# When a transposed input is turned and fetched: the feed-forward steps of an attention kernel, one step earlier

## The chip, the cores and the metric

The kernel runs on one core of one Trainium2 chip. The metric is the device time of the whole program in microseconds. A core has five engines that this text names as the profile does: PE (the matrix engine; PEld is its weight loads), DVE (the vector engine), ACT (the scalar engine), POOL (the general engine) and SP, whose only work here is to issue transfers. Each engine works through its own list of instructions in order.

## What is computed

The input `x` has the shape (2, 256, 128, 128): batch, time, frequency band, channel, all in 32-bit floats. Three residual layers follow each other, each behind a layer norm over the channels:

```python
xt = _ln(x, ln_t_w, ln_t_b).transpose(0, 2, 1, 3)
x = x + _mha(xt, t_wi, t_bi, t_wo, t_bo, H_T, cm).transpose(0, 2, 1, 3)
xf = _ln(x, ln_f_w, ln_f_b)
x = x + _mha(xf, f_wi, f_bi, f_wo, f_bo, H_F, bm)
xn = _ln(x, ln_n_w, ln_n_b)
h = jax.nn.gelu(xn @ w1.T + b1, approximate=False)
x = x + (h @ w2.T + b2)
```

The first attention runs over the 256 times of each band (causal mask), the second over the 128 bands of each time (a band mask of 16), both with four heads of 32. The feed-forward layer has 512 hidden units.

## The kernel before, in words

A test on the weights at the start picks one of two paths, and for these inputs it is `BoundedPath` (from line 877 on). Its work is cut into 384 *groups* of 512 tokens, each a tile of 128 partitions by four blocks of 128 channels: 128 groups of kind `OverTime` first, which write their result to an intermediate `x1` in device memory, and then 16 *runs*. A run is eight groups of kind `OverBands` and then eight of kind `FeedForward` on the same tokens; the middle result stays on the chip in a tile named `x2`.

The method `run` (line 1000) is a software pipeline written out by hand. It loops over a step number `n`; in each step it calls pieces of work of groups ahead of `n` and behind it. For a feed-forward group `k` the pieces are these:

- `statistics` (mean and variance, DVE) in step k-5, `root` (the inverse deviation, POOL) in step k-4.
- `normalize` and `turn` (line 1049) in step k-2. `normalize` is four DVE instructions that write `xh`; `turn` (line 504) is one DVE instruction that transposes 32 by 32 blocks into `z`, and four transfers that store `z` into a small buffer in device memory, `turned`.
- `fetch` (line 1047) in step k-1: one transfer that reads `turned` back as `xnT`, the transposed, normalized input with the channels on the partitions.
- `first_half` in step k: hidden units 0 and 1 (`hp`, two matrix products on `xnT`); `second_half`, later in step k: hidden units 2 and 3. In the first feed-forward step of a run, which the code calls the *turn*, the second half follows the first at once.
- `weigh` in step k+1: the 16 products `zp` that add up the hidden units. `divide`, in the same step: one DVE addition `res<-zp,res`, and on every second group the store to `out`.

For an `OverBands` group `k` the same pieces stand in other steps: `normalize` and `turn` in step k-3 (line 1050), `fetch` in k-2 (line 1046), the products for queries, keys and values in k-1, the scores `sp` in step k, `rp` and `op` in k+1, `yp` in k+2. Below, *band step b* and *feed step f* are the steps with `n` at the b-th band group and the f-th feed-forward group of a run, both counted from 0; *feed group f* is named in the same way.

A group's tokens come in with `load`, called for group n+11 at the head of each step (line 1024). Four groups share one tile `x` of four blocks. The transfers of the tile are issued by its first two groups, two transfers each (lines 943 and 974).

Three things decide when a piece really runs:

- The instructions of PE, DVE, ACT and POOL are pinned to the order of the program (`InOrder`, line 862). So the step that a piece is called in fixes its neighbours on its engine.
- The transfers are not pinned. The framework's scheduler puts them in an order of its own into the one list that SP works through, and an SP instruction that must wait holds all those behind it.
- Tiles come from rings of buffers: three for `xnT`, two each for `xh` and `z`, three for `turned`, four for `x`, and eight banks for what PE writes, handed out in turn. A writer waits until the last reader of the buffer's previous tile has done.

Of the kernel before, what the change touches and what calls it, by code (L numbers as in the profile page):

```python
# [25 lines left out]
NT = 4  # L26
# [623 lines left out]
def rows_of(h):  # L650
    return slice(h * D, (h + 1) * D)
# [225 lines left out]
class BoundedPath:  # L877
# [53 lines left out]
    def groups(self, x, out):  # L931
        nc, k = self.nc, self.k
        B, T, FB, C = x.shape
        NC_T = T // P
        for b in range(B):
            for f0 in range(0, FB, GA):
                held = {}


                def load(g, f0=f0, b=b, held=held):  # L940
                    if g == 0:
                        self.quad(held, "x", 4)
                    for i in range(2 * g, min(2 * g + 2, NT)):
                        f = f0 + i // NC_T * NT
                        nc.sync.dma_start(held["x"][rows_of(i)], self.of_times(x[b], i, slice(f, f + NT)))

                def store(g, f0=f0, b=b, held=held):
                    for i in range(NT if g % 2 else 0):
                        f = f0 + i // NC_T * NT + g
                        nc.sync.dma_start(  # L950
                            self.of_times(k.x1[b], i, slice(f - 1, f + 1)), held["res"][rows_of(i), :, g - 1 : g + 1]
                        )

                def part(name, g, i=None, a=0, held=held):
                    if name == "res" and name not in held:
                        self.quad(held, "res", 2)
                    if i is not None:
                        return self.longer(held[name], i * NT + g, a)
                    return held[name][:, :, g]

                for g in range(NT):
                    yield OverTime(self, partial(part, "x", g), partial(part, "res", g), partial(load, g), partial(store, g))
        for b in range(B):
            for r0 in range(0, T, RUN):
                run = []
                for t0 in range(r0, r0 + RUN, GB):
                    held = {}


                    def load(g, t0=t0, b=b, held=held):  # L970
                        if g == 0:
                            self.quad(held, "x", 4)
                            self.quad(held, "x2", 2 * RUN // GB)
                        for i in range(2 * g, min(2 * g + 2, NT)):
                            nc.sync.dma_start(
                                held["x"][rows_of(i)].rearrange("q g t c -> q (g t) c"),
                                self.of_bands(k.x1[b], t0 + NT * i, NT),
                            )

                    def store(g, t0=t0, b=b, held=held):  # L980
                        for i in range(NT if g % 2 else 0):
                            nc.sync.dma_start(
                                self.of_bands(out[b], t0 + NT * i + g - 1, 2),
                                held["res"][rows_of(i), g - 1 : g + 1].rearrange("q g t c -> q (g t) c"),
                            )

                    def part(name, g, i=None, a=0, held=held):
                        if name == "res" and name not in held:
                            self.quad(held, "res", 2)
                        if i is not None:  # L990
                            return self.longer(held[name], g * NT + i, a)
                        return held[name][:, g]

                    run += [(g, part, load, store) for g in range(NT)]
                for g, part, load, _ in run:
                    yield OverBands(self, partial(part, "x", g), partial(part, "x2", g), partial(load, g))
                for g, part, _, store in run:
                    yield FeedForward(self, partial(part, "x2", g), partial(part, "res", g), None, partial(store, g))

    def run(self, x, out):  # L1000
        groups = list(self.groups(x, out))

        def do(n, *names):
            if 0 <= n < len(groups):
                for name in names:
                    getattr(groups[n], name)()
# [4 lines left out]
        def do_at(n, kind, *names):  # L1011
            if at(n, kind):
                do(n, *names)
# [1 line left out]
        A = RUN // NT  # L1015

        self.scalar.preload_act_table_set(EXP_SET)
        for n in range(-11, len(groups) + 2):
            feeds = [at(n - 2 + i, FeedForward) for i in range(5)]
            bands = [at(n - 2 + i, OverBands) for i in range(5)]  # L1020
            turn = feeds[2] and bands[1]
            old, new = (groups[i] if at(i, OverTime) else None for i in (n, n + 1))
            self.by_columns = at(n - 1, Attention)
            do(n + 11, "load")
            if bands[2] and feeds[1]:
                self.scalar.preload_act_table_set(EXP_SET)
            do_at(n + 4, FeedForward, "root")
            do(n, "first_half", "first_function", "first_mask")
            if old is not None or new is not None:
                time_scores(old, new)  # L1030
                b = self.banks
                Attention.place = dict(rp=b["b0"], op=b["b3"], yp=b["a1"], qp=b["a2"], kp=b["b1"], vp=b["b2"])
            else:
                Attention.place = {}
            if old is not None:
                old.second_weights(old.late)
            if new is not None:
                new.first_weights(new.early)
            if old is not None:
                old.second_weights(old.early)  # L1040
                old.mask_second()
                old.add(0)
            if turn:
                do(n, "second_half", "second_function")
            do_at(n + 3, OverTime, "fetch")
            do_at(n + 2, OverBands, "fetch")
            do_at(n + 1, FeedForward, "fetch")
            do_at(n + 5, OverTime, "statistics")
            do_at(n + 2, FeedForward, "normalize", "turn")
            do_at(n + 3, OverBands, "normalize", "turn")  # L1050
            do_at(n + 4, OverTime, "normalize", "turn")
            do_at(n + 5, FeedForward, "statistics")
            do(n - 1, "weigh")
            do(n - 1, "invert_exactly" if turn else "invert")
            if new is not None:
                new.first_weights(new.late)
                new.mask_first()
            if old is not None:
                old.add(1)
            if bands[2] or turn or old is not None:  # L1060
                do(n - 2, "output", "finish")
            do(n - 1, "divide")
            if not turn:
                do(n, "second_half", "second_function")
            if not bands[2]:
                do_at(n, FeedForward, "bias")
                do_at(n + A, OverBands, "bias")
                if at(n - 1, FeedForward) and at(n - 2, OverBands):
                    do_at(n + A - 1, OverBands, "statistics", "root")
                if not turn:  # L1070
                    do_at(n + A, OverBands, "statistics")
                    if not at(n, OverTime):
                        do_at(n + A, OverBands, "root")
            do_at(n + 2, OverTime, "queries_keys", "take_query", "take_key")
            do_at(n + 1, OverBands, "queries_keys", "take_query", "take_key")
            do_at(n + 5, OverTime, "root_by_scalar", "refine")
            if at(n - 1, OverTime):
                do_at(n + A - 1, OverBands, "root_by_scalar", "refine")
            do_at(n, OverTime, "bias")
            if not bands[2] and not turn and old is None:  # L1080
                do(n - 2, "output", "finish")
            do_at(n + 2, OverTime, "values", "take_values")
            do_at(n + 1, OverBands, "values", "take_values")
            if old is not None or new is not None:

                b = self.banks
                self.banks = dict(
                    a1=b["a1"], a2=b["a2"], b0=b["a0"], b3=b["a3"], a0=b["b0"], a3=b["b1"], b1=b["b3"], b2=b["b2"]
                )
# [69 lines left out]
```

## Time and profile before

The median of three runs is 2756.72 us (2755.34 to 2758.24). The profiled execution has a span of 2755.9 us.

| engine | busy us | share |
|---|---|---|
| PE | 2695.7 | 98% |
| DVE | 2288.9 | 83% |
| POOL | 1861.0 | 68% |
| ACT | 1843.3 | 67% |

| stretch | length us | PE busy | DVE busy |
|---|---|---|---|
| start, to 40 us | 40 | 10.18 | 20.94 |
| 40 to 880: over time | 840 | 835.99 | 807.64 |
| 880 to 2700: change of kind, and the runs | 1820 | 1801.75 | 1441.74 |
| end | 56 | 47.74 | 18.61 |

| transfer | count | KB each | median us to landing |
|---|---|---|---|
| turned<-z | 1536 | 64 | 2.0 |
| xnT<-turned | 384 | 256 | 2.8 |
| x<-in_x | 128 | 256 | 5.4 |
| x<-x (from `x1`) | 128 | 256 | 4.2 |
| out<-res | 256 | 128 | 2.4 |

The 128 groups over time take until about 980 us. The first feed-forward group of the first run starts at 1045.37 us, and from there on the runs follow each other at some 109 us each; the last one, with no bands of a further run in it, takes 56 us. Because the pieces are recorded by one helper, all of them carry line 872, and the rows of the profile are told apart by the names of their tiles. A matrix product of 32-bit floats is recorded twice, so the four products `hp` of a group are eight records.

### The profile page before, as it was taken

How to read it: one execution, taken by the hardware profiler on the slowest of the kernel's cores; microseconds unless marked ns; L12 is line 12 of the kernel's file. 1: busy time of each engine (PE TensorE's matmuls, PEld its weight loads, DVE VectorE, ACT ScalarE, POOL GpSimd, SP SyncE). 2: the span in 40 equal slices, each digit the busy share in tenths (PEclk: the TensorE clock that was granted, in tenths of full speed). 3: DMA queues.
4: the chain of work that ended last, by engine and by line, in shares of the span. 5: the costliest groups of instructions: out<-in, count | busy, mean ns of one | idle time of the engine just before them, and what ended most of it. 6: DMA issues, size and time to landing. Idle time of an engine off the chain costs nothing.

```text
span 2755.9 us, 105739 instructions
## 1 busy us (share of the span) xinstructions
PE 2695.7 (98%) x43522; PEld 1880.6 (68%) x43522; DVE 2288.9 (83%) x6727; ACT 1843.3 (67%) x3600; POOL 1861.0 (68%) x2169
## 2 busy tenths in 40 slices
PE   5999999999999999999999999999999999999998
PEld 3666766667666666676676766766766767667666
DVE  5999999999999987868778778687687796776874
ACT  3888888888888874655746646557456465465563
POOL 2878878788887876666657566666566665665762
PEclk9999999999999999999999999999999999999999
DMA  5565555555555564444443544544444445344333
GB/s 126 135 154 135 148 156 141 142 154 144 148 149 144 134 157 105 109 129 108 121 127 105 129 108 109 132 115 115 129 107 122 111 114 130 103 117 113 87 97 86
DMA packets 471310, 343.84 MB, mean 125 GB/s; under 512 B 43296, under 2 KB 405152, under 8 KB 470816
## 3 DMA queue, kind: packets, MB, share of 16 engines
q1 hardware_dynamic: 469568, 335.92, 47.3%
q8 instruction: 344, 5.64, 0.9%
q14 instruction: 150, 1.23, 0.2%
q10 hardware_dynamic: 1248, 1.05, 0.1%
HBM read 169.03 MB, written 167.77 MB: 122 GB/s over the span
## 4 chain that ended last, share of the span: by engine, by line
PE 82%; DVE 11%; DMA 4%; issue 1%; SPq 1%; POOL 1%; ACT 0%; DVEq 0%
PE zp L872 17%; PE hp L872 16%; PE sp L872 10%; PE op L872 7%; PE rp L872 7%; PE vp L872 7%; PE qp L872 6%; PE kp L872 6%; PE yp L872 6%; DVE xh L872 2%; DVE vy L872 2%; DMA xnT<-turned 2%; DVE u L872 1%; DVE stats L872 1%; DVE res L872 1%
## 5 line engine op out<-in xcount | busy, mean ns | idle before, releaser
L872 ACT ACTIVATE hT<-hp,b 128x512 f32<-128x512 f32 x512 | 350.2, 687 | 553.0 <-PE hp L872 542.1
L872 POOL TENSOR_SCALAR_AFFINE_SELECT pf<-pf 128x512 f32<-128x512 f32 x768 | 476.9, 635 | 274.8 <-ACT pf L872 248.6
L872 DVE TENSOR_SCALAR xh<-x,mv,rstd 128x160 f32<-128x160 f32 x1536 | 596.2, 430 | 14.1
L872 PEld LDWEIGHTS zp<-w2T_sb,hT 128*128 128x128 f32 x4096 | 476.3, 192 | 56.2 <-issue 54.1
L872 PE MATMUL hp<-xnT,w1f 128*128 128x512 f32 x1024 | 471.2, 597 | 13.5 <-DMA xnT<-turned 11.6
L872 PE MATMUL zp<-w2T_sb,hT 128*128 128x128 f32 x4096 | 479.8, 275 | 0.1
L872 ACT ACTIVATE p<-sp 128x512 f32<-128x512 f32 (+1 forms) x1024 | 417.3, 501 | 19.9 <-PE sp L872 7.5
L872 POOL TENSOR_SCALAR_AFFINE_SELECT p<-p 128x1024 f32<-128x1024 f32 x256 | 280.2, 1095 | 199.9 <-ACT p L872 199.8
L872 PE MATMUL sp<-qT,kT 32*128 32x128 f32 (+1 forms) x8192 | 363.0, 310 | 5.4 <-DVE oT L872 3.6
L872 PEld LDWEIGHTS sp<-qT,kT 32*128 32x128 f32 x8192 | 310.7, 185 | 56.7 <-ACT kT L872 44.4
L872 PEld LDWEIGHTS vp<-wf,xnT 128*32 128x32 f32 (+1 forms) x7400 | 237.9, 113 | 153.8 <-issue 137.8
L872 POOL TENSOR_TENSOR p<-p,p 128x512 f32<-128x512 f32 x256 | 328.7, 1284 | 10.7
L872 DVE BATCH_NORM_STATS2 stats<-x 128x6 f32<-128x128 f32 x1536 | 327.6, 276 | 6.9 <-DMA x<-in_x 6.8
L872 PEld LDWEIGHTS hp<-xnT,w1f 128*128 128x128 f32 x1024 | 182.3, 191 | 191.4 <-issue 115.3
L872 ACT ACTIVATE pf<-sp 128x512 f32<-128x512 f32 x512 | 264.3, 603 | 59.2 <-PE sp L872 59.0
L872 PE MATMUL qp<-xnT,wf 128*32 128x512 f32 (+1 forms) x1850 | 267.2, 593 | 27.8 <-DMA xnT<-turned 25.8
L872 DVE STREAM_TRANSPOSE z<-xh 128x512 f32<-128x512 f32 x384 | 273.3, 712 | 15.6 <-DMA turned<-z 2.2
L872 POOL TENSOR_SCALAR rstd<-mv 128x4 f32<-128x4 f32 x248 | 56.3, 227 | 331.9 <-DVE mv L872 330.8
L872 ACT ACTIVATE qT<-qp,bq 128x512 f32<-128x512 f32 x256 | 176.0, 687 | 146.0 <-PE qp L872 146.0
L872 PE MATMUL vp<-wf,xnT 128*32 128x128 f32 (+1 forms) x7400 | 272.3, 273 | 0.0
L872 POOL TENSOR_TENSOR rstd<-rstd,mhalf 128x4 f32<-128x4 f32 x248 | 256.6, 1035 | 20.7
L872 PE MATMUL yp<-wn,oT 128*32 128x128 f32 (+1 forms) x7808 | 270.5, 273 | 0.0
(95 smaller groups left out, 4025.3 us busy)
## 6 DMA issues: line engine op xcount, KB each, us to landing
turned<-z SPq DMA_DIRECT2D x1536, 64.0 KB, 2.0
xnT<-turned SPq DMA_DIRECT2D x384, 256.0 KB, 2.8
x<-in_x SPq DMA_DIRECT2D x128, 256.0 KB, 5.4
x<-res SPq DMA_DIRECT2D x256, 128.0 KB, 3.5
x<-x SPq DMA_DIRECT2D x128, 256.0 KB, 4.2
out<-res SPq DMA_DIRECT2D x256, 128.0 KB, 2.4
w1T_sb<-in_w1T ACTq DMA_DIRECT2D x1, 256.0 KB, 4.3
w2T_sb<-in_w2T ACTq DMA_DIRECT2D x1, 256.0 KB, 4.7
```

Of the source, the lines that this page charges most:

```text
L872: return self.tc.keep_in_program_order(emit(*args, **kwargs))
```

## The change

Three edits, all in the order of the pipeline; no instruction is added to an engine or taken from it.

1. A feed-forward group is normalized and turned in step k-3 instead of k-2, as an `OverBands` group is, and fetched in step k-2 instead of k-1.
2. `load` is called for group n+12 instead of n+11, and behind the fetches of the step instead of at its head. The loop starts one step earlier for it.
3. Each of the four groups that share a tile `x` issues one of its four transfers, where the first two issued two each.

It is for a longer distance between the moment when a feed-forward input is asked for and the moment when PE needs it, for one normalization in each step throughout a run (before, one step at the change from bands to feeds had none, and one at the change back had two), and for token loads that stand behind the more urgent fetch.

```diff
                 def load(g, f0=f0, b=b, held=held):
                     if g == 0:
                         self.quad(held, "x", 4)
-                    for i in range(2 * g, min(2 * g + 2, NT)):
-                        f = f0 + i // NC_T * NT
-                        nc.sync.dma_start(held["x"][rows_of(i)], self.of_times(x[b], i, slice(f, f + NT)))
+                    f = f0 + g // NC_T * NT
+                    nc.sync.dma_start(held["x"][rows_of(g)], self.of_times(x[b], g, slice(f, f + NT)))
...
-                        for i in range(2 * g, min(2 * g + 2, NT)):
-                            nc.sync.dma_start(
-                                held["x"][rows_of(i)].rearrange("q g t c -> q (g t) c"),
-                                self.of_bands(k.x1[b], t0 + NT * i, NT),
-                            )
+                        nc.sync.dma_start(
+                            held["x"][rows_of(g)].rearrange("q g t c -> q (g t) c"),
+                            self.of_bands(k.x1[b], t0 + NT * g, NT),
+                        )
...
-        for n in range(-11, len(groups) + 2):
+        for n in range(-12, len(groups) + 2):
...
-            do(n + 11, "load")
...
             do_at(n + 3, OverTime, "fetch")
-            do_at(n + 2, OverBands, "fetch")
-            do_at(n + 1, FeedForward, "fetch")
+            do_at(n + 2, (OverBands, FeedForward), "fetch")
+            do(n + 12, "load")
             do_at(n + 5, OverTime, "statistics")
-            do_at(n + 2, FeedForward, "normalize", "turn")
-            do_at(n + 3, OverBands, "normalize", "turn")
+            do_at(n + 3, (OverBands, FeedForward), "normalize", "turn")
             do_at(n + 4, OverTime, "normalize", "turn")
```

## The prediction

> **What bounds the kernel now.** I read the page first, then the waits of PE, then the timeline around the places where PE waits.
>
> ```profile
> span 2755.9 us, 105739 instructions
> PE 2695.7 (98%) x43522; PEld 1880.6 (68%) x43522; DVE 2288.9 (83%) x6727; ACT 1843.3 (67%) x3600; POOL 1861.0 (68%) x2169
> L872 PE MATMUL hp<-xnT,w1f 128*128 128x512 f32 x1024 | 471.2, 597 | 13.5 <-DMA xnT<-turned 11.6
> ```
>
> PE is idle for 60 us in all, 30 of them in the first 40 us and 8 at the end; so 22 us can be won between. The row of `hp` names the place: its idle time is put down to the fetch of `xnT`. The waits of PE say how often:
>
> ```profile
> PE qp L872 <- DMA xnT<-turned: 25.8, 1, 25.8
> PE hp L872 <- DMA xnT<-turned: 11.6, 14, 2.1
> PE sp L872 <- DVE oT L872: 3.6, 1, 3.6
> ```
>
> The columns are total us, times, longest. The first is the start of the program, the third the change from the time layer to the runs at 980 us; neither has a feed-forward group in it. The second is what the change can touch. The timeline at the head of a feed-forward phase shows it:
>
> ```profile
> 2238.64 1.60 DVE L872 TENSOR_SCALAR xh<-x,mv,rstd 128x160 f32<-128x160 f32 x4
> 2240.28 0.71 DVE L872 STREAM_TRANSPOSE z<-xh 128x512 f32<-128x512 f32 x1
> 2241.02 2.74 SPq L514 DMA_DIRECT2D turned<-z  x4
> 2245.14 0.34 SPq L519 DMA_DIRECT2D xnT<-turned  x1
> 2245.94 1.06 PE L872 MATMUL yp<-wn,oT 128*32 128x128 f32 x32
> 2248.00 2.38 PE L872 MATMUL hp<-xnT,w1f 128*128 128x512 f32 x5 [1.01 <-DMA xnT<-turned]
> ```
>
> Feed group 0 is normalized at 2238.64, one band step (6.44 us) before PE wants it. Normalizing, transposing, storing, waiting for the store and fetching take 9.2 us up to 2247.86. PE ends its list of the band step first. All 16 feed-forward phases start in this race; by the starts of their records PE came first, and waited, in 14.
>
> How much it costs is read from the distance between the heads of the runs (the first `hp` of feed group 0), two of them here:
>
> ```profile
> 2028.99:2137.38 108.39, 108.39 (x1441) 75.85 (x1441) 84.14 (x254) 62.48 (x104) 68.55 (x95) 1.00 0.46 118
> 2248.00:2358.73 110.73, 108.47 (x1440) 75.85 (x1441) 86.31 (x264) 64.41 (x105) 70.65 (x99) 1.00 0.45 117
> ```
>
> The columns are length, then busy time of PE, PEld, DVE, ACT, POOL. PE's work is the same; the first run has no wait at all, the second has 2.3 us of it. From 1045.37 to 2687.28 there are 15 distances, 1641.91 us together. A run without a wait takes 108.38. So 1641.91 - 15 x 108.38 = 16.2 us of the 15 runs are waits, or their consequences; the head of the first run, before 1045.37, adds 0.86 (from the start of the last `yp` to `hp` 1.85 us, against 0.99 where PE does not wait). Together **17.1 us**.
>
> I sorted the 17 us by the place in the run, from the starts of the matrix products in the trace. The step into feed group 0 holds 12.4; the first half of feed group 1 1.4; a step in the middle of the feeds, where the fetch stood in SP's list behind a store of four transfers, 2.0; and 1.7 is a slower clock: after its longest wait, 2.1 us before 2358.73, the eight `hp` took 5.37 us instead of 3.68, and the granted clock in 2357 to 2361 was 0.77.
>
> **What the Trainium skill says.** On the clock, "TensorE: Matmul & The Clock Gate", section "What's actually happening": the default state is throttled and activity releases it, to half rate after an idle window of about 3.4 us. The trace agrees in kind: waits of 1.0 us at 2248.00 left the clock at 1.00, the one of 2.1 us had a slower clock behind it. On the round trip, "DMA: Bandwidth & Descriptors", section "Anatomy of one DMA — SWDGE (gpsimd) path": about 2 us of a transfer are fixed, most of it the confirmation that the last byte has landed, and the wait for a semaphore is made by the issuing engine, not by the transfer. Here the transfers are issued by SP, but the numbers are close: 2.0 us for the 64 KB stores, 2.8 us for the 256 KB fetch. So store and fetch cannot be shortened; only an earlier start hides them. The second half of that sentence is why SP's list matters below.
>
> **The change, part by part.**
>
> *Turned one step earlier.* In its list PE has 6.4 us of work in a band step and 7.0 in a feed step (3.44 for `hp` plus 3.57 for `zp`). Feed group 0's `xh` moves from band step 6 to band step 5, so from about 2129.07 to 2122.83 in the run that ends at 2137.38. That is 6.2 us more than before against waits of at most 2.1 us. Every later feed group gains a step in the same way: all 17.1 us should go, with a margin of 4 us for the worst of them.
>
> *What DVE pays.* No instruction is new; one `xh` (four instructions, 1.60 us) and one `z` (0.71) move in each run from feed step 5, which had two sets, to band step 5, which had none. With their gaps they take 2.27 us. DVE's slack in that step:
>
> ```profile
> 2124.62 0.69 DVE L872 TENSOR_TENSOR x<-yp,x 128x512 f32<-128x512 f32 x1 [0.65 <-PE yp L872]
> 2128.46 0.70 DVE L872 TENSOR_TENSOR sp<-sp,band 128x512 f32<-128x512 f32 x1 [1.09 <-PE sp L872]
> ```
>
> 0.65 + 1.09 = 1.74 us. The step then lasts 6.53 us on DVE, like its neighbours (2128.46 to 2135.00), and the next begins at 2122.23 + 6.53 = 2128.76, 0.30 later than before. From there DVE has no gap until it has done `oT` of band 7, so everything to that point is 0.30 us later. Who waits for it? The exponential of the fourth head in band step 7 starts 0.52 us after DVE's mask addition has ended: hidden. `yp` of band 6 starts 1.15 us after its `oT`, that of band 7 1.14 us: hidden. The tightest is a PSUM bank:
>
> ```profile
> 2148.07 0.63 DVE L872 TENSOR_TENSOR x<-yp,x 128x512 f32<-128x512 f32 x1
> 2149.18 1.88 PE L872 MATMUL hp<-xnT,w1f 128*128 128x512 f32 x4
> ```
>
> The second half of feed group 1 writes the bank from which DVE reads `yp` of band 6, by the order in which banks are handed out. DVE is done at 2148.70 and PE starts at 2149.18; 0.48 - 0.30 leaves 0.18 us. In a run that waits, the slack is larger now (up to 3.1 us), but without waits all runs will look like this one. I take it as hidden, at 0; if release and start need more than 0.18 us between them, it costs some 0.1 to 0.3 us a run, up to 5 in all.
>
> *Fetched one step earlier, and the wait this adds.* Three buffers hold `xnT`, so the fetch of feed group f now needs the buffer of feed group f-3, free only when PE has done that group's second half, at the end of feed step f-3. In the built order of the changed program, SP's list has each fetch right behind its own four stores, or behind a store to `out`, as before. So the fetch can stop SP for some 4 to 6 us, until the feed step ends. Behind it stand the stores to `out` (nobody waits for them until the two buffers of `res` have gone round, a run later) and the next group's stores to `turned`, whose `z` is made only in the next step. After the wait the fetch needs 2.8 us and its input is read two steps, 14 us, later. For band groups 0 and 1 of the next run the buffers are those of feed groups 5 and 6, and the reader comes one step after the release: 7 us against 2.8. Cost 0.
>
> *Loads.* In the built order SP's list is the same as before up to the first feed-forward phase, and within the runs the loads keep their places between the same stores and fetches; the scheduler had already moved them many steps ahead of where they are called (one load issues at 2091.94, as soon as DVE has left the buffer, two runs ahead). DVE, ACT, POOL and PE have the same lists outside the moved pieces. So both load edits cost and bring 0, and the 980 us over time stay as they are.
>
> Sum: 2756.7 - 17.1 - 0 = **2739.6 us**.
>
> **The rivals.**
>
> 1. *All waits go, nothing comes back* (70 in 100): 2739.6, with the scatter of the three times (3 us) and small waits below 0.1 us that may go too: 2736 to 2742.
> 2. *Part is given back at the change of kind* (16): DVE's 0.30 us make PE wait for the bank, or for the exponentials, by 0.3 to 0.6 us in each of 16 runs: 5 to 10 us, so 2745 to 2750. For it speaks that DVE is without a gap for 24 us there; against it, the slacks above.
> 3. *The wait takes another form* (8): the fetch for the first bands comes late, or SP's list holds a later one up, so that the runs stay near 109.4 us: 2752 to 2760. Against it: the margin of 4 us each.
> 4. *Slower* (6): SP, held by a fetch that waits for its buffer, passes that on to the next stores at each of the eight feed steps, and 0.1 us for each of 128 groups is 13 us: 2769. Against it: SP is idle for more than a third of each step in the timeline, and the next `z` is not there earlier.
>
> **How the numbers follow.** The likeliest case gives 2739.6. The range is from 2736 (the small waits also gone) to 2750 (the far end of the second rival); what is left out is the third and the fourth. Faster by over 0.2% (5.5 us) are the first two cases, 0.86; within 0.2% the third, 0.08; slower 0.06.
>
> **What would show it.** The waits of PE must lose the row "hp from xnT" (11.6 us) and keep the others. The heads of all 16 runs must lie 108.4 us apart. On DVE, band step 5 must have no gap and feed step 5 a single `xh`; the addition `sp` of band step 6 must follow on 6.5 us after that of step 5. The waits of SP at line 519 must grow on PE `hp`, which is harmless. The stretch up to 980 us must have its old length; if it differs, the loads did something. The prediction is wrong if PE gets a new row of waits at `hp` for DVE `x`, or if a first `qp` of a run waits for its fetch.

## The result, and the profile after

The changed kernel takes 2746.57 us (2745.24 to 2746.85), the kernel before, on the same chip, 2757.11: a ratio of 0.9961, with an interval from 0.9944 to 0.9979. That is 10.5 us gained, where 17.1 were forecast. The time lies inside the range that was given, but in the second rival's stretch (2745 to 2750) and not in the likeliest case.

The page of the profiled execution after the change, the lines that answer to those shown of before:

```profile
span 2743.3 us, 105749 instructions
PE 2691.9 (98%) x43522; PEld 1881.9 (69%) x43522; DVE 2284.3 (83%) x6727; ACT 1841.5 (67%) x3600; POOL 1860.9 (68%) x2169
L872 PE MATMUL hp<-xnT,w1f 128*128 128x512 f32 x1024 | 469.2, 596 | 0.0
```

The idle time before `hp` was 13.5 us and is 0.0: not one feed-forward product waits for its input any more. The waits of PE (total us, times, longest), however, have a row that was not there:

```profile
PE qp L872 <- DMA xnT<-turned: 26.5, 2, 26.3
PE rp L872 <- DVE u L872: 4.3, 16, 0.3
```

Sixteen times 0.3 us, once in each run: `rp` waits for a DVE instruction that writes `u`. The timeline of one run shows where (start, length, engine, line, operation, tiles):

```profile
2131.73 0.83 DVE L872 BATCH_NORM_STATS2 stats<-x 128x6 f32<-128x128 f32 x4
2132.47 0.36 DVE L872 BATCH_NORM_AGGREGATE mv<-stats 128x2 f32<-128x6 f32 x4
2132.75 0.66 DVE L872 TENSOR_TENSOR x<-yp,x 128x512 f32<-128x512 f32 x1
2133.33 0.69 DVE L872 TENSOR_TENSOR rp<-rp,r 128x512 f32<-128x512 f32 x1
2134.05 0.69 DVE L872 SCALAR_TENSOR_TENSOR u<-rp,r 128x512 f32<-128x512 f32 x1
```

```profile
2130.93 3.70 PE L872 MATMUL hp<-xnT,w1f 128*128 128x512 f32 x8
2134.89 1.07 PE L872 MATMUL rp<-pf,ones 128*32 128x512 f32 x8 [0.25 <-DVE u L872]
```

This is feed step 0. PE has made `hp` of feed group 0 at once, then wants to write the sums `rp` of band 7, and starts them 0.15 us after DVE's `u` has ended (2134.05 + 0.69 = 2134.74). That `u` reads the `rp` of band 6. The code says why one waits for the other: in a band step ten PSUM banks are handed out, four for `sp` and six for `yp`, `qp`, `rp`, `op`, `kp` and `vp`. In the last band step there is no next band, so `kp` and `vp` are not asked for; only eight are handed out up to the next `rp`, there are eight banks, and `rp` of band 7 falls on the bank of `rp` of band 6.

The stretches of both profiles, by the heads of the runs (length, then busy time of PE, PEld, DVE, ACT, POOL). First the 15 runs before, then after:

```profile
1045.37:2687.28 1641.91, 1629.19 (x21600) 1138.02 (x21601) 1277.72 (x3839) 951.27 (x1560) 1043.45 (x1439) 1.00 0.44 115
```

```profile
1043.59:2674.50 1630.91, 1626.92 (x21604) 1139.37 (x21600) 1275.09 (x3841) 949.85 (x1561) 1044.22 (x1441) 1.00 0.46 115
```

The heads lie 108.71 to 108.80 us apart now, in every run; before, it was 108.38 to 110.73. So the scatter of the waits has gone, and each run is 0.34 us longer than the quietest run before. The stretch up to the first head is 1.8 us shorter, of which 0.86 is the wait that was forecast there; the last stretch, from the last head to the end, takes 68.8 us instead of 68.6. (The 56 us that were given for the last run above are only its part behind 2700 us.)

### The profile page after: what moved, and what is told of

The parts are those of the page before. It is cut to its first block, busy times and chain, and to the rows that moved or that the text cites. A ratio compares the mean times of both kernels' runs of the same rounds, so it can differ in the third digit from the quotient of the medians.

```text
span 2743.3 us, 105749 instructions
## 1 busy us (share of the span) xinstructions
PE 2691.9 (98%) x43522; PEld 1881.9 (69%) x43522; DVE 2284.3 (83%) x6727; ACT 1841.5 (67%) x3600; POOL 1860.9 (68%) x2169
## 4 chain that ended last, share of the span: by engine, by line
PE 79%; DVE 15%; DMA 3%; issue 1%; SPq 1%; ACT 0%; POOL 0%; DVEq 0%
PE zp L872 17%; PE hp L872 14%; PE sp L872 10%; PE op L872 8%; PE rp L872 7%; PE vp L872 6%; PE qp L872 6%; PE kp L872 6%; PE yp L872 6%; DVE xh L872 3%; DVE stats L872 2%; DVE z L872 2%; DVE u L872 2%; DVE rp L872 2%; DMA xnT<-turned 2%; DVE sp L872 1%
## 5 line engine op out<-in xcount | busy, mean ns | idle before, releaser
L872 DVE TENSOR_TENSOR res<-zp,res 128x512 f32<-128x512 f32 x128 | 87.4, 683 | 236.4 <-PE zp L872 236.4
```

The source lines that it names most:

```text
L872: return self.tc.keep_in_program_order(emit(*args, **kwargs))
```

## The experiments

Theory 1: what was not gained is the wait of `rp` for a bank, and DVE reaches `u` 0.30 us later because of the normalization that was moved into band step 5. Theory 2: the rest was lost elsewhere and the wait only shows it. Theory 3: behind the bank of `rp` stands another, as tight. The first four kernels ran on one chip, beside the kernel before at 2757.67 us; the last four on one chip beside it at 2756.7.

**The changed kernel again**, unchanged, as the measure.

> The changed kernel once more, as the measure for the other kernels on the same chip. Both theories: 2746 us, 10 to 11 below the kernel before; heads of the runs 108.72 us apart; 16 waits of 0.3 us of rp for u.

Measured: 2746.51 us, ratio 0.9959 (0.9946 to 0.9973); heads 108.72 us apart, `rp` for `u` 4.3 us in 16 waits. As expected.

**Other banks for `rp` and `op` in the turn.** No instruction is added or moved.

```diff
         path.held = dict(yp=path.turn_of_bank(), qp=path.turn_of_bank())
-        self.rp = path.bank([P, NT * P], "rp")
+        self.rp = path.bank([P, NT * P], "rp", path.held["qp"] if path.turning else None)
...
                 path.tensor.matmul(self.op[r, c], self.v[:, i, r], self.p[:, h, i, :], start=True, stop=True)
+        if path.turning:
+            path.turn_of_bank()
...
             turn = feeds[2] and bands[1]
+            self.turning = turn
```

> The changed kernel, but in the first feed-forward step of a run the sums rp of band 7 go to the bank that is set aside for the queries and is not used there, and op to the bank that rp had. Theory 1 (what was not gained is the wait of rp for the bank that DVE reads as rp of band 6 until its instruction u, made 0.30 us later by the moved normalization): the 16 waits of 0.3 us go, heads 108.4 us apart, 5 to 6 us below the changed kernel, about 2741. Theory 2 (the rest was lost elsewhere, in transfers or in the time layer, and the wait only shows it): within 1.5 us of the changed kernel. Theory 3 (the next bank, that of yp of band 6, is as tight): a new wait of hp for DVE x of 0.1 to 0.3 us, and 1 to 4 us gained.

Measured: 2741.15 us (2740.28 to 2742.16), ratio 0.9941 (0.9927 to 0.9954), 5.4 us below the changed kernel. The heads are 108.38 us apart. `rp` begins before DVE's `u` has ended, and PE waits for nothing in the 15 runs, by the stretches:

```profile
2024.27 0.69 DVE L874 SCALAR_TENSOR_TENSOR u<-rp,r 128x512 f32<-128x512 f32 x1
2024.78 1.06 PE L874 MATMUL rp<-pf,ones 128*32 128x512 f32 x8
```

```profile
1045.70:2671.45 1625.75, 1625.75 (x21605) 1137.92 (x21601) 1275.28 (x3841) 949.38 (x1561) 1044.34 (x1441) 1.00 0.45 116
```

DVE is as late as in the changed kernel; only the bank differs. So the bank carried the loss, and theories 2 and 3 fall. This version is faster than both kernels of the case.

**Less work for DVE in band step 5.** The band mask of the fourth head of that one band group is made by POOL.

```diff
+            if bands[2]:
+                groups[n].by_vector = 0 if at(n + 3, FeedForward) and not at(n + 2, FeedForward) else 1
             do(n, "first_half", "first_function", "first_mask")
```

> The changed kernel, but in band step 5 the band mask of the fourth head is made by POOL (two more selections of 0.64 us) instead of DVE (one addition, 0.61 us from start to start). Theory 1: DVE has 0.61 us less where it lacked 0.53 (2.27 against 1.74 of slack), so u of band 6 is as early as before, the wait of rp shrinks from 0.36 to about 0.06, 4 to 5 us below the changed kernel, about 2742. Theory 2: within 1.5 us of the changed kernel. A rival for this kernel alone: POOL, idle for 1.4 us in a band step, is 1.3 us later and PE waits at rp of band 5 for the mask; then slower than the changed kernel by up to 1 us in each of 16 runs.

Measured: 2741.41 us (2740.24 to 2742.63), ratio 0.9941 (0.9928 to 0.9955), 5.1 us below the changed kernel. Heads 108.43 us apart; the row of `rp` for `u` is gone, and `rp` follows 3.68 us after the start of `hp`, against 3.96 in the changed kernel and 3.66 in the quiet run before. The POOL rival did not come. The loss therefore needs both: DVE's lateness and the shared bank.

**More work for DVE in band step 5.**

```diff
             do_at(n + 3, (OverBands, FeedForward), "normalize", "turn")
+            if at(n + 3, FeedForward) and not at(n + 2, FeedForward):
+                self.vector.tensor_scalar(self.spare, self.spare, 1.0, None, ALU.mult)
...
         tc.nc.vector.memset(self.eps, EPS)
+        self.spare = once.tile([P, NT * P], F32, name="spare")
+        tc.nc.vector.memset(self.spare, 0.0)
```

> The changed kernel with one more DVE instruction in band step 5 of each run, a multiplication by one of a spare 128x512 tile, behind the normalization (about 0.43 us, as oT<-u of the same shape takes). Theory 1: there is no slack left, so each run is longer by all of it: the wait of rp for u grows from 0.36 to about 0.8, 16 x 0.43 = 7 us above the changed kernel, about 2753. Theory 2: DVE's lateness is hidden, within 1.5 us of the changed kernel.

Measured: 2752.17 us, ratio 0.9981 (0.9974 to 0.9989), 5.7 us above the changed kernel; heads 109.05 to 109.15 us apart, that is 0.33 more, where 0.43 were expected. The size of the dose was wrong, not the mechanism: from its start to the next instruction's start the added one takes 0.30 us, and from the second instruction behind it on DVE's list is 0.33 us later than in the changed kernel. The 0.43 was read from the length of a record.

```profile
2014.66 0.38 DVE L872 TENSOR_SCALAR spare<-spare 128x512 f32<-128x512 f32 x1
2014.96 0.86 DVE L872 BATCH_NORM_STATS2 stats<-x 128x6 f32<-128x128 f32 x4
```

All of the dose arrives, but in two places: `rp` starts 0.16 us later behind `hp`, and the scores `sp` of bands 6 and 7 take 0.08 and 0.09 us more each. So theory 1's "all of it in the wait of `rp`" is not exact; a second brake stands close behind the first. By the count of the banks it is this: the scores of the third head take the bank of the `yp` of three bands before, which DVE reads in its `x<-yp,x`.

```profile
2022.55 0.66 DVE L872 TENSOR_TENSOR x<-yp,x 128x512 f32<-128x512 f32 x1
2023.16 1.26 PE L872 MATMUL sp<-qT,kT 32*128 32x128 f32 x32
```

In the changed kernel this `x` has ended 0.12 to 0.30 us before the scores of bands 6 and 7 begin. Here it ends 0.04 to 0.14 us after their beginning, and their third record starts 0.05 to 0.06 us behind that end, for both bands in all 16 runs. No kernel here moves that bank, so this is read from the trace and the code and not tested.

**Both: other banks and the extra instruction.** The edits are the two above.

> The other banks and the extra DVE instruction of 0.33 us in band step 5 together. Theory (behind the bank of rp the next bound is the bank of yp of band 6, which hp of feed group 1 takes 0.05 us after DVE has read it): PE waits there instead, for DVE x, by about 0.3 to 0.4 us in each of 16 runs, 5 to 6 us above the kernel with other banks, about 2746. Rival (with other banks DVE has slack again): within 1.5 us of the kernel with other banks, 2741.

Measured: 2743.41 us, ratio 0.9950 (0.9936 to 0.9964), heads 108.57 us apart: 0.19 more than with other banks alone. Neither expectation holds. The new time is in the scores again, 1.26 us from first start to last end instead of 1.17. And the bank that the prediction named as the tightest is not one:

```profile
2032.75 0.63 DVE L874 TENSOR_TENSOR x<-yp,x 128x512 f32<-128x512 f32 x1
2033.37 1.88 PE L874 MATMUL hp<-xnT,w1f 128*128 128x512 f32 x4
```

`hp` begins at 2033.37, before DVE has finished reading `yp` at 2033.38. It does not wait for that bank, here or at any other of the 16 heads (0.01 to 0.03 us before the end of `x`). The list of waits names no reader that holds the scores up; their third record again starts 0.06 us behind the end of DVE's `x`, in all 16 runs.

**The turn earlier, the fetch as before.** Of the change only this, without the fetch and the loads:

```diff
-            do_at(n + 2, FeedForward, "normalize", "turn")
-            do_at(n + 3, OverBands, "normalize", "turn")
+            do_at(n + 3, (OverBands, FeedForward), "normalize", "turn")
```

> The kernel before with feed-forward groups normalized and turned in step k-3, as in the change, but fetched in step k-1 and with the loads as before. Theory 1 (what counts is when z is made; the scheduler puts a fetch right behind its stores wherever it is called): as the changed kernel, 2746 us, no wait of hp for xnT, the 16 waits of rp for u. Rival (the earlier call of the fetch is what hides it): waits of hp for xnT stay, 2750 us or more.

Measured: 2745.5 us, ratio 0.9962 (0.9950 to 0.9975), heads 108.70 to 108.80 us apart, `rp` for `u` 4.3 us in 16 waits, no wait of `hp`. The whole effect of the change is in this one edit. The earlier call of the fetch brings nothing that can be measured, and it is hardly a change: of SP's 2692 transfers it puts one fetch in each of 15 runs ahead of the next group's four stores, and all the rest stand in the same order, by the names of their tiles.

**The loads alone.** The edits of `load` and of its place, with the feed-forward steps as before:

```diff
-        for n in range(-11, len(groups) + 2):
+        for n in range(-12, len(groups) + 2):
...
-            do(n + 11, "load")
...
             do_at(n + 1, FeedForward, "fetch")
+            do(n + 12, "load")
```

> The kernel before with the two load edits alone. Its lists of instructions are those of the kernel before on every engine and on SP, so both theories expect the kernel before within its scatter: 2755 to 2760 us, and the same 11 to 12 us of waits of hp for xnT.

Measured: 2756.9 us against 2756.7, ratio 1.0001 (0.9993 to 1.0009). Its waits of `hp` for `xnT` are 11.0 us. The loads do nothing: SP's 2692 transfers stand in the same order as in the kernel before, by the same names.

**The kernel before with other banks.** The edit is that of the other banks.

> The kernel before with the other banks for rp and op of band 7. Theory 1 (there the bank is no bound, since PE waits for xnT and DVE has caught up): within 2 us of the kernel before, 2757; the waits of hp for xnT stay at about 12 us. Rival (the bank costs PE in both kernels): 4 us or more below it.

Measured: 2758.79 us, ratio 1.0005 (0.9996 to 1.0013), waits of `hp` for `xnT` 14.5 us, where about 12 were expected. Before the change the bank is hardly a bound: in the profile of the kernel before, `u` had ended 0.20 us or more before `rp` began at 14 of the 16 heads, and 0.15 us before at the other two.

## Why the prediction was right and where it was wrong

*The 17.1 us of waits: right.* The row "hp from xnT" is gone, with other banks the kernel gains 16.5 us, and its 15 runs take 1625.75 us, 15 times 108.38, which is what the prediction had read off the quietest run before (1625.7). (The parts into which it sorted the 17 us add up to 17.5, so that sorting is good to 0.4 us.) The slow eight `hp` behind the longest wait are gone with it: at all 16 heads of the changed kernel they take 3.70 us, none 5.37. For how the clock works this case has only that one event. The wait ahead of it, 2.1 us, is shorter than the idle window of about 3.4 us that the prediction quotes, and in the kernel before with other banks a wait of 1.90 us had a granted clock of 1.00 around and behind it.

*DVE's share: right in size.* Measured, the additions `sp` of band steps 5 and 6 start at 2115.79 and 2122.32, the forecast 6.53 apart, with no gap between, and feed step 5 has a single `xh`. In feed step 0 `u` ends 3.81 us after the first `hp` (2130.93 to 2134.74), against 3.51 in the quiet run before.

*"Who waits for it?": this step failed.* It listed the exponential, the two `yp` and one bank, and called that bank the tightest with 0.48 us. It left out the bank of `rp`. The quiet run that it leaned on had the answer in view: there `rp` started 3.66 us after `hp`, 0.06 more than the 3.60 of the shortest run, and 0.15 us behind the end of `u` (2140.20 + 0.69).

```profile
2137.38 3.68 PE L872 MATMUL hp<-xnT,w1f 128*128 128x512 f32 x8
2140.20 0.69 DVE L872 SCALAR_TENSOR_TENSOR u<-rp,r 128x512 f32<-128x512 f32 x1
2141.04 1.06 PE L872 MATMUL rp<-pf,ones 128*32 128x512 f32 x8
```

The list of waits has no row for so short a delay, but 0.15 us is also the distance at all 16 heads of the changed kernel, where PE does wait. So there was no slack at all. 0.06 + 0.30 makes 0.36 us in each of 16 runs, 5.8 us; the measured difference of the heads is 0.34, and 5.4 us came back with other banks. The bank that the prediction named was also the wrong one: counting the order again, the output of band 7 takes its bank only behind the second half, so `yp` of band 6 shares with the last product of that half, which starts 0.86 us later.

*The second rival had the size and half of the mechanism* ("make PE wait for the bank, or for the exponentials, by 0.3 to 0.6 us in each of 16 runs"), at 16 in 100. A bank it was, and 0.34 us a run, but not the bank that it meant: its sign, a new row of waits at `hp` for DVE `x`, did not come. The cause for the low chance is the missing item in the list of slacks. That the time fell inside the range is partly luck: the range reached to 2750 for the sake of a wait at another bank, and the working of the likeliest case was 7.0 us too low.

*The fetch and its new wait: the cost of 0 was right, the size of the wait was not.* The waits of SP at line 519 for PE `hp` grew from 21.3 to 34.6 us, but the longest is 1.4 us as before, where stops of 4 to 6 us were thought possible, and with the turn alone they are already 30.0 us. Nobody waits for them: no `qp` of the runs has a gap of 0.05 us or more before it. *The loads: right*, by the kernel that has them alone.

*What is not settled:* the first head came 0.9 us earlier than the forecast wait accounts for. Kernels with the same lists up to there had it between 1043.59 and 1045.70 us, so this is scatter and not an effect.

## What to carry to other kernels

When a wait is removed from the busiest engine, ask what else that engine would have waited for at the same place: an earlier arrival uses up the slack of every other condition there, and a bank or buffer that is free "just in time" becomes the next bound. Count the ring of buffers at the places where the pattern changes (a last step without its usual requests), since two tiles that never share a buffer in the steady state may do so there. And where an engine is without a gap for many instructions, even 0.3 us of moved work goes through to its far end.

## What the runs showed of the hardware that was not expected

A DVE `tensor_scalar` on 128x512 in place, whose record lasts 0.38 us, put the next instruction's start 0.30 us behind its own in a full list and made the list behind it 0.33 us later; the length of a record overstates such a dose. The end of DVE's `u` and the start of the PE product `rp` that takes its bank lie 0.15 us apart, both before the change (2140.89 to 2141.04) and after it (2134.74 to 2134.89). This distance is not one for all: between the end of DVE's `x` and the third record of the scores it was 0.05 to 0.06 us.
